# Three rotating PSUM banks for up products and a piece's products, one bank for products back and turned rows, in a fused selective-scan and mixture-of-experts kernel

## The chip, the core and the metric

The kernel runs on one core of a Trainium2 chip. The engines that matter are TensorE (PE, with its weight loads as PEld), VectorE (DVE), ScalarE (ACT), GpSimd (POOL, which here only issues indirect DMAs) and SyncE (SP, which issues plain DMAs). Each runs its own list of instructions in order and waits on semaphores for the others. TensorE writes only into PSUM; in this kernel PSUM is used as eight banks, each 128 partitions by 512 float32 numbers. The metric is the device time of one execution in microseconds; the median of three runs is given, and one more execution was profiled.

## The reference

The input x has 2 batches of 2048 tokens of 256 numbers. After a layer norm the output is the input plus two branches:

```
xn  = layernorm(x)
# branch 1: a selective scan over tokens sorted by their nearest of 8 means
buckets = argmax(normalized xn . normalized means)     # order = stable sort by bucket
u    = xn in that order, transposed                    # (B, 256, L)
dts, Bm, Cm = split(x_proj_weight @ u);  Cm += prompt of the bucket
delta = softplus(dt_projs_weight @ dts + bias)
h_t  = exp(delta_t * A) * h_{t-1} + (delta_t * u_t) * B_t      # 256 x 16 states
y_t  = sum over states of h_t * C_t + D * u_t          # put back in the old order
# branch 2: top 2 of 8 experts for each token
out  = sum over the two experts of p * (silu(xn @ w1) * (xn @ w3)) @ w2
x + branch 1 + branch 2
```

## The kernel before

**Front.** The rows of x are loaded, turned (`turn_rows`, L376: for each group of 512 tokens one half goes through a bank of pool `ps_m`, the other through `ps_t`, L379), scored against the 16 columns of means and gate weights (`by_chooser`, two banks of pool `ps_h`), normalised and written to a scratch tensor in DRAM. Tokens are routed to experts and sorted by bucket; `list_tokens` (L310) turns positions into lists of row numbers with products into the tile `pl`.

**Two streams of work, interleaved by hand.** After the front, two streams share the engines.

The *scan stream* has 8 pieces of 512 tokens (2 batches of 4). A piece has 8 steps (4 groups of 4 states, by 2 halves of the 256 channels), so there are 64 steps, and a step has 4 places. At a place VectorE multiplies du by B into `bu` (`feed`, L840) and runs one scan of 512 steps into `hs` (`scan`, L849), while ScalarE makes a decay `da` for the step after it (L834). TensorE works one step behind: at places 1 and 2 it turns the finished `hs` (`turn`, L861, into two banks of `ps_t`; ScalarE copies them out as `ht`, L865), and at place 3 it contracts with `z`, which holds C, into the two accumulators `y0` and `y1` (L870, the two banks of `ps_s`). Before a piece can begin, its rows are gathered, turned (`Piece.turn`, tile `pt_u`, L653), projected (`project` and `end_projection`, tile `px`, L667 and L674), and its step sizes made (`size`: products into two tiles `pd`, L714, then eight ScalarE passes into `e` and `r`, L732). All of this is done during the piece before it, at fixed places: `turn` at place 2 and 3 of that piece's step 1, `project` in two calls at places 1 and 3 of step 2, `end_projection` at place 0 of step 3, and `size` behind the first product back that is dealt from place 2 of step 3 on. `decay_of_one`, `log` and `series` (L734 to L757) follow in steps 4 to 7; `log` loads ScalarE's table for the logarithm.

The *expert stream* has 68 tiles of 128 token slots that are dealt among the places (three more tiles stand in a branch at the end, L1208, which this input doesn't take). A tile's rows are gathered by an indirect DMA (`load_rows`, L928), turned (`Tile.turn`, tile `pt_g`, L937, copied out as `xT`, L939), multiplied up by w1 and w3 (`up(0)` and `up(1)`, 16 products each into one bank, L954), gated on VectorE (`silu`, L967, after ScalarE's tanh, L962; `gate`, L971), multiplied back (`down`, tile `py`, L977), scaled on ScalarE (`yo`, L981) and added to the output by an indirect DMA (L895). Weights come by indirect DMAs too (L914), three tiles ahead. `Tile.turn` also makes `own`, each row's share, with two small VectorE instructions.

**PSUM.** `ps_s` has two banks (y0, y1), `ps_t` two (pt_s, and half of the front's turned rows). `ps_h` has one bank for each of two tags: `h0` for the product `up(0)` and `h1` for `up(1)`. `ps_m` has two banks that everything else shares in turn: `pt_g`, `py`, `pt_u`, `px`, `pd` and the small products of the front.

**The dealer.** The expert stream is a list of jobs: `up(0)` and `up(1)` of tile t, then `down` of tile t - 1, and so on (L1067 to L1072). Just before `down(t)` the job also turns the rows of tile t + 2 (`turn_tile`). The first seven jobs (`lead`, L1078) surround the first piece's preparation. The others are dealt in the loop over places: each place carries an estimate of its TensorE and VectorE time (`on_pe`, `on_dve`), and a job, at `PART` and `PART_DVE`, is given as soon as TensorE's sum falls behind a fixed ratio of VectorE's. A silu or gate is recorded two places after its product, in `later`; `vector_work(t)` records at once all that is left of tiles up to t. `part_up(t)` calls it for t - 1 before its products, `part_down(t)` for t. Finally `keep_order` fixes each engine's instructions in the order in which they were recorded.

Of the kernel before, what the change touches and what calls it, by code (L numbers as in the profile page):

```python
# [39 lines left out]
F32 = mybir.dt.float32  # L40
# [5 lines left out]
PSUM = bass.MemoryType.PSUM  # L46
DRAM = bass.MemoryType.DRAM

P = 128
# [7 lines left out]
def scan_moe_kernel(  # L57
# [46 lines left out]
    ps_t = ctx.enter_context(tc.tile_pool(name="ps_t", bufs=2, space=PSUM))  # L104
    ps_h = ctx.enter_context(tc.tile_pool(name="ps_h", bufs=1, space=PSUM))
    ps_m = ctx.enter_context(tc.tile_pool(name="ps_m", bufs=2, space=PSUM))
    front = ctx.enter_context(ExitStack())
# [193 lines left out]
    def first_of_max(v, m, i):  # L301
# [6 lines left out]
        nc.vector.tensor_reduce(i, c, AX.X, ALU.min)  # L308

    def list_tokens(place, of_batch, width: int, tag: str, factors, between=()):  # L310

# [10 lines left out]
        lo, hi = lo_hi  # L322
        pl = ps_m.tile([P, 2, width], F32, tag="m", name="pl")
        for m in range(n // LC):
# [41 lines left out]

    by_chooser = [ps_h.tile([P, CH], F32, tag=f"h{b}", name="by_chooser") for b in range(B)]
    scores = [ps_s.tile([P, JC, JC, G], F32, tag=f"y{b}", name="scores") for b in range(B)]
# [269 lines left out]
    class Piece:  # L638
# [9 lines left out]
        def turn(self, h: int):  # L648
            if h == 0:
                self.u = pre.tile([P, ND, CH], F32, tag="tok", name="u")  # L650
            pt = ps_m.tile([P, JC, P], F32, tag="m", name="pt_u")
            for i in range(JC):
                nc.tensor.transpose(pt[:, i, :], self.xs[:, i, h * P : (h + 1) * P], ident)  # L653
            nc.scalar.copy(self.u[:, h, :], pt.rearrange("p i t -> p (i t)"))
# [8 lines left out]
        def project(self, h: int):  # L663
            if h == 0:
                self.px = ps_m.tile([2 * XP, HC], F32, tag="m", name="px")
            for t in range(2):
                nc.tensor.matmul(  # L667
                    self.px[t * XP : (t + 1) * XP, :], lhsT=xpT[:, h, :],
                    rhs=self.u[:, h, t * HC : (t + 1) * HC], start=h == 0, stop=False,
                )  # L670
# [38 lines left out]
        def size_products(self):  # L709

            self.pd = [ps_m.tile([P, ND, HC], F32, tag="m", name="pd") for _ in range(2)]
            for h in range(ND):
                for t in range(2):
                    nc.tensor.matmul(  # L714
                        self.pd[t][:, h, :], lhsT=dtT[t * XP : t * XP + R, h * P : (h + 1) * P],
                        rhs=self.xd[t * XP : t * XP + R, :], start=True, stop=True,
                    )
# [191 lines left out]
    class Tile:  # L909
# [37 lines left out]
        def up(self, i: int):  # L947
            wk = w13_sb[self.t % NW][:, i * ND * H : (i + 1) * ND * H].rearrange(
                "p (h f) -> p h f", h=ND
            )  # L950
            p = ps_h.tile([P, NH, TS], F32, tag=f"h{i}", name=f"p{i}_ps")
            for f in range(NH):
                for h in range(ND):
                    nc.tensor.matmul(  # L954
                        p[:, f, :], lhsT=wk[:, h, f * P : (f + 1) * P], rhs=self.xT[:, h, :],
                        start=h == 0, stop=h == ND - 1,
                    )
            if i == 0:

                self.p1 = p  # L960
                self.s = ffn.tile([P, NH, TS], F32, tag="t", name="t_sb")
                nc.scalar.activation(self.s, p, AF.Tanh, scale=0.5)  # L962
            else:
                self.p3 = p
# [70 lines left out]
    def vector_work(t: int):  # L1035

        for when in sorted(later):
            later[when] = [(u, do) for u, do in later[when] if u > t or do()]

    def part_up(t: int, i: int):  # L1040
        def do():
            vector_work(t - 1)
            tiles[t].up(i)
# [5 lines left out]
    def part_down(t: int):  # L1049
        def do():  # L1050
            if t + 2 < n_dealt:
                turn_tile(t + 2)
            vector_work(t)
# [14 lines left out]
    for t in range(n_dealt + 1):  # L1068
        if t < n_dealt:
            jobs += [part_up(t, 0), part_up(t, 1)]  # L1070
        if t > 0:
            jobs.append(part_down(t - 1))  # L1072
    turn_tile(0)
    turn_tile(1)
# [42 lines left out]
    for n, p in enumerate(pieces):  # L1117
# [3 lines left out]
        if n:  # L1121
# [4 lines left out]
            for h in range(ND):  # L1126
                at_place(s1 + 1, 2 + h, lambda p=p, h=h: p.turn(h), 0.5)
                at_place(s1 + 2, 1 + 2 * h, lambda p=p, h=h: p.project(h), 0.55)
                at_place(s1, 18 + 2 * h, lambda p=p, h=h: p.decay_of_one(h))
# [21 lines left out]
    for n in range(NSUB * len(steps)):  # L1151
        on_dve[n] += 1.75
        if n >= NSUB:
            on_pe[n] += (0.0, 0.9, 0.9, 1.1)[n % NSUB]
    PART, PART_DVE = 2.05, 0.5
    left = len(jobs) - ahead
    ratio = (sum(on_pe[:n_places]) + left * PART) / (sum(on_dve[:n_places]) + left * PART_DVE)
    pe_now = dve_now = 0.0
    for k in range(len(steps)):
        step = steps[k]  # L1160
        before_ = steps[k - 1] if k else None
        for i in range(NSUB):
# [22 lines left out]
            while given < len(jobs) and (  # L1185
                pe_now + PART / 2 < ratio * dve_now or place + 1 >= n_places
            ):
                jobs[given]()
                given += 1
                pe_now += PART  # L1190
                dve_now += PART_DVE
                size_now()
# [89 lines left out]
```

## Time and profile before

| what | value |
|---|---|
| median of three runs | 751.91 us (751.2 to 751.93) |
| the profiled execution | 752.28 us |
| its span, first to last instruction | 750.5 us |
| mean granted TensorE clock | 0.951 |
| first bu of the scan stream | 98.66 us |
| end of the last dealt scan on VectorE | 735.2 us |

In the lists of waits a line names who waited, for what, and then the microseconds in total, how often, and the longest. In a timeline a line has its start, the time it spans, the engine, the source line, what was written from what, and how many like instructions are merged into it; the bracket at its end is idle time of that engine just before, with what ended it. In the table of stretches there follow, after the stretch and its length, busy time and instructions (x) of each engine, the granted clock, the DMA share and GB/s.

### The profile page before, as it was taken

The numbers are of one execution on the slowest core, as the hardware profiler recorded it, in microseconds if no ns is written. First come the engines' busy times: TensorE is split into PE (matmuls) and PEld (weight loads), VectorE is DVE, ScalarE is ACT, GpSimd is POOL, SyncE is SP. The second block draws the span as 40 slices with busy tenths as digits, with TensorE's granted clock in tenths as the row PEclk, the third lists the DMA queues.
The fourth block names the chain that finished last, engine by engine and source line by source line (L and its number), as shares of the span: only waits on it lengthen the run. The fifth ranks groups of instructions, "written<-read, shape, count | busy, mean of one in ns | idle before, by whom it ended". The sixth has DMA issues, their size and how long they took to land.

```text
span 750.5 us, 16877 instructions
## 1 busy us (share of the span) xinstructions
PE 678.0 (90%) x6506; PEld 588.9 (78%) x6506; DVE 678.5 (90%) x1085; ACT 508.0 (68%) x983; POOL 523.0 (70%) x362
## 2 busy tenths in 40 slices
PE   7375779999998999999999999999999998999993
PEld 5144678888877998888878898999798977899982
DVE  8885389899987999999999999999999997999991
ACT  4830446686758866886769577967795768767762
POOL 2023448667777788777877887788788888887733
PEclk9755979999999999999999999999999999999996
DMA  8676544584436755685458656865575547745312
GB/s 269 243 162 233 166 162 92 159 244 138 124 56 171 252 146 117 171 264 148 114 132 281 160 130 124 255 198 132 119 249 157 128 93 219 227 125 118 86 17 29
DMA packets 60401, 120.31 MB, mean 160 GB/s; under 512 B 24160, under 2 KB 41248, under 8 KB 53152
## 3 DMA queue, kind: packets, MB, share of 16 engines
q0 software_dynamic: 38784, 63.71, 36.0%
q1 hardware_dynamic: 21536, 55.50, 21.9%
q8 instruction: 52, 0.85, 0.5%
q14 instruction: 29, 0.24, 0.1%
HBM read 170.78 MB, written 22.28 MB: 257 GB/s over the span
## 4 chain that ended last, share of the span: by engine, by line
PE 69%; ACT 11%; DVE 9%; DMA 5%; issue 4%; POOL 1%; POOLq 0%; ACTq 0%; DVEq 0%
PE p_ps L954 29%; PE py L977 13%; PE pt_s L861 11%; PE y L870 7%; DMA w<-in_w_down_dram,w_row 3%; ACT ht L865 3%; PE y L796 2%; PE pl L342 2%; PE pt_g L937 2%; DMA out_dram<-yo,token_of 2%; ACT da L834 2%; DVE st L374 1%; ACT e L732 1%; ACT r L732 1%; PE px L667 1%
## 5 line engine op out<-in xcount | busy, mean ns | idle before, releaser
L954 PE MATMUL p_ps<-xT,w 128*128 128x128 f32 x2176 | 272.6, 281 | 12.3 <-DVE g L971 8.1
L954 PEld LDWEIGHTS p_ps<-xT,w 128*128 128x128 f32 x2176 | 258.0, 195 | 26.3 <-DVE g L971 8.3
L849 DVE TENSOR_TENSOR_SCAN hs<-da,carry,bu 128x512 f32<-128x512 f32 x192 | 246.0, 1281 | 0.0
L834 ACT ACTIVATE da<-dl,na 128x512 f32<-128x512 f32 x256 | 183.7, 734 | 0.2 <-DVE dl L789 0.2
L840 DVE TENSOR_TENSOR bu<-du,bt 128x512 f32<-128x512 f32 x256 | 173.1, 676 | 0.0
L865 ACT COPY ht<-pt_s 128x512 f32<-128x512 f32 x256 | 138.4, 595 | 40.3 <-PE pt_s L861 39.3
L895 POOL DMA_INDIRECT out_dram<-yo,token_of x68 | 131.4, 1932 | 48.0 <-ACT yo L981 22.6
L914 POOL DMA_INDIRECT w<-in_w_up_dram,w_row x68 | 91.8, 1350 | 89.2 <-DVE w_row L595 43.4
L861 PE MATMUL pt_s<-ident,hs 128*128 128x128 f32 x1024 | 136.8, 277 | 9.7 <-ACT ht L865 8.6
L977 PE MATMUL py<-w,g 128*128 128x256 f32 x544 | 129.8, 381 | 7.5 <-ACT xT L939 4.8
L861 PEld LDWEIGHTS pt_s<-ident,hs 128*128 128x128 f32 x1024 | 116.5, 142 | 21.4 <-ACT ht L865 13.4
L977 PEld LDWEIGHTS py<-w,g 128*128 128x128 f32 x544 | 98.0, 190 | 20.6 <-ACT xT L939 6.0
L928 POOL DMA_INDIRECT xg_sb<-xn,token_of x68 | 91.8, 1349 | 26.2 <-issue 12.8
L914 POOL DMA_INDIRECT w<-in_w_down_dram,w_row x68 | 94.7, 1392 | 20.7 <-issue 13.4
L895 POOL DMA_INDIRECT out_dram<-yt,line_of x32 | 66.1, 2065 | 23.0 <-issue 11.3
L849 DVE TENSOR_TENSOR_SCAN hs<-da,bu 128x512 f32<-128x512 f32 x64 | 78.1, 1221 | 0.0
L962 ACT ACTIVATE t_sb<-p_ps 128x512 f32<-128x512 f32 x68 | 41.0, 603 | 54.5 <-PE p_ps L954 54.4
L870 PE MATMUL y<-ht,z 128*32 128x128 f32 x2048 | 74.0, 277 | 1.5 <-PEq L1208 0.7
L981 ACT ACTIVATE yo<-py,own 128x256 f32<-128x256 f32 x68 | 32.3, 475 | 61.4 <-PE py L977 58.8
L967 DVE SCALAR_TENSOR_TENSOR t_sb<-t_sb,p_ps 128x512 f32<-128x512 f32 x68 | 45.8, 674 | 26.1 <-ACT t_sb L962 26.1
L870 PEld LDWEIGHTS y<-ht,z 128*32 128x32 f32 x2048 | 50.8, 109 | 19.6 <-issue 10.2
L632 POOL DMA_INDIRECT xs<-xn,line_of x32 | 41.8, 1306 | 14.7 <-issue 8.2
(202 smaller groups left out, 582.0 us busy)
## 6 DMA issues: line engine op xcount, KB each, us to landing
bt<-bc SPq DMA_DIRECT2D x31, 1024.0 KB, 5.1
z<-bc SPq DMA_DIRECT2D x32, 256.0 KB, 3.2
xn<-xt SPq DMA_DIRECT2D x8, 520.0 KB, 2.6
xt<-in_x_dram SPq DMA_DIRECT2D x8, 512.0 KB, 8.0
out_dram<-in_x_dram SPq DMA_DIRECT2D x8, 512.0 KB, 8.3
w<-in_w_up_dram,w_row POOLq DMA_INDIRECT x68
w<-in_w_down_dram,w_row POOLq DMA_INDIRECT x68
xg_sb<-xn,token_of POOLq DMA_INDIRECT x68
```

The source lines that it names most:

```text
L834: nc.scalar.activation(self.da[i], self.piece.dl[:, self.h, :], AF.Exp, scale=na[:, self.h, n : n + 1])
L840: nc.vector.tensor_mul(self.bu[i], self.piece.du[:, self.h, :], self.piece.bts[self.q][:, i, :])
L849: nc.vector.tensor_tensor_scan(self.hs[:, :, i], self.da[i], self.bu[i], start, ALU.mult, ALU.add)
L861: nc.tensor.transpose(pt[:, j, :], self.hs[:, t0 : t0 + G, :].rearrange("p t n -> p (t n)"), ident)
L865: nc.scalar.copy(self.ht[i], pt)
L870: nc.tensor.matmul(p.ys[self.h][j * G : (j + 1) * G, i, :], lhsT=p.zs[q][:, i * (P // G) + j, :], rhs=self.ht[i][:, j, :], start=False, st ...
L895: ins = nc.gpsimd.indirect_dma_start(out=out_rows, out_offset=bass.IndirectOffsetOnAxis(ap=numbers, axis=0), in_=rows, in_offset=None, com ...
L914: nc.gpsimd.indirect_dma_start(out=to[self.t % NW], out_offset=None, in_=rows, in_offset=bass.IndirectOffsetOnAxis(ap=w_row[:, self.t : se ...
L928: nc.gpsimd.indirect_dma_start(out=self.xg, out_offset=None, in_=xn_d, in_offset=bass.IndirectOffsetOnAxis(ap=token_of[:, self.t : self.t ...
L954: nc.tensor.matmul(p[:, f, :], lhsT=wk[:, h, f * P : (f + 1) * P], rhs=self.xT[:, h, :], start=h == 0, stop=h == ND - 1,)
L967: nc.vector.scalar_tensor_tensor(self.s, self.s, 1.0, self.p1, ALU.add, ALU.mult)
L977: nc.tensor.matmul(py, lhsT=self.g[:, f, :], rhs=w2[:, f, :], start=f == 0, stop=f == NH - 1)
```

## The change

`ps_h` becomes one ring of three banks under a single tag `h`. Besides the up products it takes `pt_u`, `px`, both `pd` tiles and `pl`; the front's two `by_chooser` tiles come from it as well. `ps_m` shrinks to one bank, which is left to `pt_g`, `py` and the small or turned tiles of the front.

A list `taken` remembers which tile's product lies in each of the three banks. `take_bank`, called ahead of every allocation from the ring, records all silu and gate work up to the tile whose product lay in the bank that now comes round. `part_up` no longer calls `vector_work` itself.

The rows of tile t + 1 are turned just before `up(1)` of tile t; before, those of tile t + 2 were turned just before `down(t)`. Both calls of `project` move to place 0 of step 3, next to `end_projection`. The dealer's estimates are replaced: a place's VectorE time, TensorE's three places, and a job's time, which now differs for up products and products back. A job's own time decides when it is given.

```diff
-    ps_h = ctx.enter_context(tc.tile_pool(name="ps_h", bufs=1, space=PSUM))
-    ps_m = ctx.enter_context(tc.tile_pool(name="ps_m", bufs=2, space=PSUM))
+    ps_h = ctx.enter_context(tc.tile_pool(name="ps_h", bufs=3, space=PSUM))
+    ps_m = ctx.enter_context(tc.tile_pool(name="ps_m", bufs=1, space=PSUM))
...
+    taken = [-1] * 3
+    vector_work_to = [lambda t: None]
+
+    def take_bank(t: int = -1):
+        vector_work_to[0](taken.pop(0))
+        taken.append(t)
...
-        pl = ps_m.tile([P, 2, width], F32, tag="m", name="pl")
+        pl = ps_h.tile([P, 2, width], F32, tag="h", name="pl")
+        take_bank()
...
-            pt = ps_m.tile([P, JC, P], F32, tag="m", name="pt_u")
+            take_bank()
+            pt = ps_h.tile([P, JC, P], F32, tag="h", name="pt_u")
...
-                self.px = ps_m.tile([2 * XP, HC], F32, tag="m", name="px")
+                take_bank()
+                self.px = ps_h.tile([2 * XP, HC], F32, tag="h", name="px")
...
-            self.pd = [ps_m.tile([P, ND, HC], F32, tag="m", name="pd") for _ in range(2)]
+            self.pd = []
+            for _ in range(2):
+                take_bank()
+                self.pd.append(ps_h.tile([P, ND, HC], F32, tag="h", name="pd"))
...
-            p = ps_h.tile([P, NH, TS], F32, tag=f"h{i}", name=f"p{i}_ps")
+            take_bank(self.t)
+            p = ps_h.tile([P, NH, TS], F32, tag="h", name=f"p{i}_ps")
...
+    vector_work_to[0] = vector_work
+
     def part_up(t: int, i: int):
         def do():
-            vector_work(t - 1)
+            if i == 1 and 1 < t + 1 < n_dealt:
+                turn_tile(t + 1)
             tiles[t].up(i)
...
     def part_down(t: int):
         def do():
-            if t + 2 < n_dealt:
-                turn_tile(t + 2)
             vector_work(t)
             tiles[t].down()
...
+    UP, DOWN, GATE, OWN = 2.0, 2.4, 0.67, 0.36
+    job_pe = [DOWN if n % 3 == 1 and n > 1 else UP for n in range(len(jobs))]
...
-                at_place(s1 + 2, 1 + 2 * h, lambda p=p, h=h: p.project(h), 0.55)
+                at_place(s1 + 3, 0, lambda p=p, h=h: p.project(h), 0.55)
...
-        on_dve[n] += 1.75
+        on_dve[n] += 1.95
         if n >= NSUB:
-            on_pe[n] += (0.0, 0.9, 0.9, 1.1)[n % NSUB]
-    PART, PART_DVE = 2.05, 0.5
-    left = len(jobs) - ahead
-    ratio = (sum(on_pe[:n_places]) + left * PART) / (sum(on_dve[:n_places]) + left * PART_DVE)
+            on_pe[n] += (0.0, 1.07, 1.07, 1.14)[n % NSUB]
+    left = sum(job_pe[ahead:])
+    left_dve = (len(jobs) - ahead) * (2 * GATE + OWN) / 3
+    ratio = (sum(on_pe[:n_places]) + left) / (sum(on_dve[:n_places]) + left_dve)
...
-                pe_now + PART / 2 < ratio * dve_now or place + 1 >= n_places
+                pe_now + job_pe[given] / 2 < ratio * dve_now or place + 1 >= n_places
             ):
                 jobs[given]()
+                pe_now += job_pe[given]
+                dve_now += (2 * GATE + OWN) / 3
                 given += 1
-                pe_now += PART
-                dve_now += PART_DVE
```

More of the change, by code (lines that the diff above doesn't have):

```diff
@@ L363, in late_factors @@
         return one, num
-    by_chooser = [ps_h.tile([P, CH], F32, tag=f"h{b}", name="by_chooser") for b in range(B)]
+    by_chooser = [ps_h.tile([P, CH], F32, tag="h", name="by_chooser") for b in range(B)]
     scores = [ps_s.tile([P, JC, JC, G], F32, tag=f"y{b}", name="scores") for b in range(B)]
```

## The prediction, made before the changed kernel had run

> **What bounds the kernel now.** I read five views in this order: the page's head, stretches of the dealt region, who waits on VectorE, who waits on TensorE, and the timeline around the longest waits.
>
> ```profile
> span 750.5 us, 16877 instructions
> PE 678.0 (90%) x6506; PEld 588.9 (78%) x6506; DVE 678.5 (90%) x1085; ACT 508.0 (68%) x983; POOL 523.0 (70%) x362
> ```
>
> Two engines stand at 90% of the span, so the stretches must tell which one ends the work.
>
> ```profile
> core 0: us, PE busy (x) PEld busy (x) DVE busy (x) ACT busy (x) POOL busy (x), PEclk, DMA share, GB/s
> ...
> 210.00:260.00 50.00, 45.80 (x429) 39.55 (x429) 42.03 (x59) 36.87 (x72) 39.07 (x24) 0.97 0.61 165
> ...
> 460.00:510.00 50.00, 49.88 (x506) 45.63 (x506) 49.59 (x71) 39.59 (x78) 40.97 (x27) 1.00 0.72 211
> ...
> 610.00:660.00 50.00, 46.05 (x461) 39.34 (x460) 44.29 (x61) 36.53 (x72) 42.07 (x27) 1.00 0.70 190
> ```
>
> Some stretches have both engines full (460 to 510); in others both lose time together (210 to 260, 610 to 660). VectorE's losses have one name:
>
> ```profile
> DVE t_sb L967 <- ACT t_sb L962: 26.1, 14, 4.4
> ...
> DVE one L327 <- PE pl L342: 3.2, 2, 2.3
> ```
>
> silu (L967) waits for the tanh (L962), which waits for an up product (L954). In VectorE's timeline the waits from the first scan's bu (98.7 us) to the last scan's end (735.2 us) are: 1.66 and 0.41 (silu and gate at 109 and 110), 2.31 and 0.99 (list_rows(1) at 133 and 136), 0.37, 0.31 and 0.34 (149, 190, 197), 3.26 (224), 4.43 (241), 1.32 (318), 2.05 (395), 0.84 (546), 1.61 (621), 3.82 (636): 23.7 us. Two of them:
>
> ```profile
> 224.44 0.69 DVE L967 SCALAR_TENSOR_TENSOR t_sb<-t_sb,p_ps 128x512 f32<-128x512 f32 x1 [3.26 <-ACT t_sb L962]
> ...
> 241.47 0.69 DVE L967 SCALAR_TENSOR_TENSOR t_sb<-t_sb,p_ps 128x512 f32<-128x512 f32 x1 [4.43 <-ACT t_sb L962]
> ```
>
> Start to start, VectorE takes 0.60 for a bu, 1.19 for a scan, 0.60 for a silu or gate and 0.31 for a tile's two own. One piece is 32 x 1.79 = 57.3, plus 8.2 tiles (197 dealt parts / 3 / 8) x 1.51 = 12.4, plus 7.2 of masks, series and members: 76.9 us. TensorE in the same way: a step 2 x 0.87 + 1.01 = 2.75, a tile 2 x 1.89 + 1.75 + 0.22 = 5.75, a piece's products 5.6; so 22.0 + 47.2 + 5.6 = 74.8 us. The pace is VectorE's, but TensorE has only 2.1 us a piece to spare, so each microsecond that TensorE waits soon returns as a silu that comes late. Without any VectorE wait the span would be 750.5 - 23.7 = 726.8: the floor.
>
> TensorE's own waits:
>
> ```profile
> PE pt_s L861 <- ACT ht L865: 8.6, 17, 2.2
> ...
> PE p_ps L954 <- DVE g L971: 8.1, 1, 8.1
> ...
> PE py L977 <- ACT xT L939: 4.8, 5, 1.4
> PE p_ps L954 <- ACT xT L939: 3.9, 5, 1.1
> PE py L977 <- ACT u L654: 2.6, 3, 1.2
> ```
>
> ```profile
> 98.19 3.78 PE L954 MATMUL p_ps<-xT,w 128*128 128x128 f32 x16 [8.07 <-DVE g L971]
> ```
>
> ```profile
> 215.79 0.38 PE L937 MATMUL pt_g<-ident,xg_sb 128*128 128x128 f32 x2
> 217.62 1.99 PE L977 MATMUL py<-w,g 128*128 128x256 f32 x8 [1.45 <-ACT xT L939]
> ```
>
> While px holds one of two ps_m banks (L665 to L679), the product back must take the bank of the rows just turned, and waits for ScalarE's copy. At 98 us the second up bank is held by tile 1's gate, which VectorE reaches only after the first piece's step sizes.
>
> **The change, part by part.**
>
> *Up products on three banks.* An up product now waits for the silu or gate three allocations back. In the first parts, pt_u's second half takes the bank of tile 1's first product, so silu and gate of tile 1 are forced ahead of it, into a time when VectorE idles (8.5 us before w, L775). The product of 98.19 then needs pd0's bank, whose last reader is the third of the four step-size r on VectorE, near 91.9: it starts 6.3 us sooner. The 1.66 + 0.41 at 109 go: -2.1. Gate 1 also leaves VectorE's way before the first bu (97.46): -0.6.
>
> The row at 98.19 shows 3.78 us for 16 matmuls, after 8.07 us without work and at a granted clock of 0.50; warm they take 1.95. The Trainium skill (TensorE: Matmul & The Clock Gate, Part 1) puts the drop at an idle window of about 3.4 us; the wait left would be some 1.9 us, so by it the product stays warm and saves 1.8 more. TensorE is already early there, so the sum is the same by either.
>
> *A piece's products leave ps_m; both project calls go to one place.* The py waits of 4.8 + 2.6 go. Piece by piece upstream of a VectorE wait: 1.45 at 129 (ahead of list_rows' products, ready before 131.5 but started at 132.75: takes 1.2 of 3.3); 1.22 + 1.45 at 206 and 217 (2.7 of 3.26); 0.72 at 297 (of 1.32); 0.71 at 375 (of 2.05); 0.65 at 526 (of 0.84); 0.70 + 0.46 at 603 and 615 (1.2 of 1.61). Sum: -7.2. Moving project (0.58 each) past other TensorE work adds none; its bank is held for some 2 us, not 10.
>
> *Rows turned one part sooner.* An xT copy now has a whole up product (1.89) ahead of its use, so the 3.9 us of up products waiting for xT go; one, 1.09 at 171, lies ahead of the three small waits: -0.7 of 1.0. On POOL's queue the row load (mean 1.35) now stands ahead of the up-weight load instead of behind it; both serve three tiles later, and TensorE waits for no weight or row DMA in this trace, so nothing; uncovered it is 1.35 a tile. own comes earlier on VectorE with the same 0.31; its rows are three tiles old. SP's queue keeps its order.
>
> *One bank for rows turned and products back.* Each is now separated from the other by an up product. From pt_g's start to the copied xT was 1.8 us at 215.79; pt_g plus an up product is 2.1. So it is hidden by 0.3, save where ScalarE loads the logarithm's table and runs it (1.28 + 1.06 at 251 us): there py comes 0.9 late, seven times, 6.3 us of TensorE. I take 0, as VectorE's series (four of 1.12 a piece) lies there and no wait stands between 250 and 315. Bounds: 0 and +6.3.
>
> The Trainium skill (PSUM — Partial Sum Buffer, Summary: rules for kernel authors) speaks against this part: reading a product while a matmul runs wants another bank. By it each of some 132 handoffs is in series, and only the order, not the bank, can hide it. The row at 217.62 agrees with the rule: 1.45 us where nothing lay between.
>
> *Front.* pt_x's first halves share one bank. TensorE must wait for ScalarE's copy (0.51 start to start) before every second tile: about 0.4 in each of three bursts, ahead of the normalising, which lies on the chain: +1.3 (bounds 0 and 3). At 70 us the second pt_g waits for the first copy, and pt_u stands behind a third: +0.9 until the first bu.
>
> *A size's gate forced sooner; parts dealt by new costs.* Walking both planners, 168 of 197 parts keep their place, 27 move by one, two by two; a place is 2.4 us and silu waits two places, so 0. Where size follows, pd's second bank can pull a gate one place forward: at most one silu distance, 1.1 us in piece 2, which the next silu then doesn't lose: 0, bounds 0 and +5. ScalarE's eight step-size passes (232.68 to 235.7), which hold ht back by 2.16 and make the 4.43 and 3.82, stay: 0.
>
> **Sum.** -2.1 - 0.6 - 7.2 - 0.7 + 1.3 + 0.9 = -8.4: span 742.1. The profiled execution took 752.28, 1.8 around its span, and 0.4 above the median 751.91. So 742.1 + 1.8 - 0.4 = 743.5; I say 743.
>
> **Rivals.**
>
> *More comes than was counted (13%).* TensorE is six microseconds early from the start and up products have a bank to run ahead in; nearly every silu is on time. For it: 2.1 us a piece to spare. Against it: the 2.16 of step-size passes is untouched. Only list_rows' 2 remain of 23.7, with the front's +2.2: about 731.
>
> *The waits move (15%).* VectorE runs dry at the next late silu or forced gate, and only the lead and list gain: -2.1 - 0.6 - 1.2 + 2.2 = -1.7: 750. For it: the two longest waits come from ScalarE, and the copy chain is longer now.
>
> *Slower: the one bank binds (22%).* Place: py behind xT and pt_g behind yo, two handoffs a tile over 66 tiles, on a ScalarE that also carries da and ht in order. Removed TensorE waits are 4.8 + 2.6 + 3.9 + 8.1 = 19.4, so from 0.3 us a tile TensorE is later than before. At 0.5 it loses 33, 14 more than it gained: 752 + 14 = 766; at 0.4, 759. For it: the hidden margin is just 0.3. Against it: in this trace ScalarE waits for py 59 times out of 68 (58.8 us), so it is seldom behind.
>
> That the third bank doesn't do what it says can be excluded but for a part: up products waited for a bank once only (8.1), so in the steady part its worth lies in freeing ps_m.
>
> **How the numbers follow.** The forecast's case has 50% and a range of its own of 735 to 748. Less than 0.2% (1.5 us) can't be told from no change. Faster: 50 + 13 and half of the case at 750: 71%. Same: the rest of it: 8% with a little of the slower one. Slower: 21%. The range takes in the case at 750 and the milder half of the slower one, and leaves out most of the case at 731: 734 to 757.
>
> **What would show it.** Right: no py wait on xT or u left, no 8 us wait at 98, silu's 26.1 near 15, the two waits after the step sizes still there, the first bu 1 to 2 us later. Wrong: py waiting on xT or pt_g on yo in most tiles (the slower case), silu's wait unchanged, or a front later by over 3 us.

## The result, and the profile after

| | before | after |
|---|---|---|
| median | 751.98 us (751.2 to 753.19, 6 runs) | 756.2 us (752.82 to 759.47, 6 runs) |
| ratio after / before | | 1.0058, 95% interval 1.0036 to 1.0080 |
| span of the profiled execution | 750.5 us | 755.0 us |
| first bu | 98.66 us | 100.77 us |
| end of the last dealt scan | 735.17 us | 738.07 us |

The changed kernel is 0.6% slower; 743 us and a gain of 1.2% were forecast. Here and below medians are of all executions, while ratios with their intervals leave out the slow ones, over 1.5% above the fastest of the same kernel.

The page's head and the three stretches shown of before, in the kernel after:

```profile
span 755.0 us, 16857 instructions
PE 677.1 (90%) x6506; PEld 592.8 (79%) x6506; DVE 679.3 (90%) x1085; ACT 508.2 (67%) x983; POOL 516.1 (68%) x362
```

```profile
210.00:260.00 50.00, 45.80 (x431) 39.92 (x429) 45.20 (x63) 37.72 (x73) 36.40 (x24) 0.97 0.63 173
460.00:510.00 50.00, 47.29 (x475) 43.20 (x475) 47.07 (x68) 37.23 (x74) 38.27 (x26) 0.97 0.72 205
...
610.00:660.00 50.00, 45.91 (x437) 40.63 (x436) 42.68 (x58) 38.53 (x75) 38.75 (x26) 0.97 0.65 182
```

From 210 to 260 VectorE gained three microseconds (42.03 to 45.20 busy). From 460 to 510, where both engines had been full, each now loses about 2.6, and the granted clock is no longer 1.00. So the change gains early and loses late. The start of the first scan of some steps says where (from VectorE's timeline in three traces; the third kernel, with one edit to the changed one, is explained under the experiments):

```
step                          0       4      12      36      48      52      60   last end
before                     99.86  145.65  227.42  466.13  585.04  622.34  703.59   735.17
after                     101.97  144.79  225.01  461.08  583.73  624.50  706.49   738.07
after, gather sooner      101.24  143.84  224.01  460.25  580.55  615.76  696.60   728.22
```

After is 2.1 us late at step 0 and 5.05 us early at step 36: 7.2 gained in the first half. By step 60 it is 2.9 us late. The waits of the whole execution, in the columns of before:

```profile
DVE t_sb L982 <- ACT t_sb L977: 26.1, 14, 4.9
...
PE pt_s L875 <- ACT ht L879: 11.2, 20, 2.6
...
PE py L992 <- ACT xT L953: 4.7, 6, 1.4
...
PE pt_u L663 <- DMA xs<-xn,line_of: 4.3, 1, 4.3
...
PE p_ps L969 <- DMA w<-in_w_up_dram,w_row: 2.1, 1, 2.1
...
DVE one L336 <- PE pl L351: 1.8, 2, 0.9
...
PE p_ps L969 <- DVE r L792: 1.6, 1, 1.6
```

What was to vanish has mostly vanished: the 8.1 us of an up product waiting for a gate, the 3.9 of up products waiting for xT, the 2.6 of py waiting for u. VectorE's wait for tanh is as long as before, and two names are new, both DMAs: TensorE waits for a piece's gathered rows (xs) and for a tile's up weights (w). The first of them, in TensorE's timeline:

```profile
599.35 0.49 PE L663 MATMUL pt_u<-ident,xs 128*128 128x128 f32 x3
604.16 0.48 PE L663 MATMUL pt_u<-ident,xs 128*128 128x128 f32 x1 [4.31 <-DMA xs<-xn,line_of]
...
607.34 2.61 PE L992 MATMUL py<-w,g 128*128 128x256 f32 x8
```

and in VectorE's, where the next silu then misses its place:

```profile
606.49 1.28 DVE L863 TENSOR_TENSOR_SCAN hs<-da,carry,bu 128x512 f32<-128x512 f32 x1
612.40 0.69 DVE L982 SCALAR_TENSOR_TENSOR t_sb<-t_sb,p_ps 128x512 f32<-128x512 f32 x1 [4.64 <-ACT t_sb L977]
```

VectorE's 4.64 us is put down to ScalarE's tanh. Followed back it is the DMA: tanh waited for an up product, which stood behind pt_u in TensorE's order. GpSimd's timeline shows when the rows were asked for:

```profile
595.33 1.25 POOL L641 DMA_INDIRECT xs<-xn,line_of  x1 [0.30 <-issue]
596.89 1.48 POOL L641 DMA_INDIRECT xs<-xn,line_of  x1 [0.31 <-issue]
598.67 1.61 POOL L909 DMA_INDIRECT out_dram<-yo,token_of  x1 [0.30 <-ACT ht L879]
600.59 1.38 POOL L928 DMA_INDIRECT w<-in_w_down_dram,w_row  x1 [0.30 <-issue]
602.28 1.40 POOL L942 DMA_INDIRECT xg_sb<-xn,token_of  x1 [0.31 <-issue]
```

Here one indirect DMA follows another with 0.30 us between them and nothing else. The last gather leaves GpSimd at 598.37, one microsecond before TensorE begins to turn its rows. The queue was no better in the kernel before: there the last gather left at 597.84, and TensorE came later, at 600.72. Even so the trace of before held a warning, small enough to be missed:

```profile
600.72 0.49 PE L653 MATMUL pt_u<-ident,xs 128*128 128x128 f32 x3
601.51 0.33 PE L653 MATMUL pt_u<-ident,xs 128*128 128x128 f32 x1 [0.30 <-DMA xs<-xn,line_of]
```

The lead of that gather over its use was 2.9 us before and 1.0 after. That is 1.9 of the 4.0 us by which the wait grew. The rest lies behind GpSimd: the rows were there 5.8 us after the gather had left it (598.37 to 604.16), against 3.7 before (597.84 to 601.51). In between stands another transfer, `bt<-bc`, a plain load of 1024 KB for the scan stream. SyncE issued it at these times, before and then after:

```profile
598.83 0.33 SPq L703 DMA_DIRECT2D bt<-bc  x1
```

```profile
597.58 0.33 SPq L714 DMA_DIRECT2D bt<-bc  x1
```

Before, the last gather left GpSimd 1.0 us ahead of this load; after, 0.8 us behind it, since the scan stream had come forward and the gather had not. The view of the DMA queues of the kernel after, from 598.40 to 601.00, has one queue alone, that of SyncE's plain DMAs (GpSimd's is q0; the line has packets, megabytes, share of the 16 DMA engines' time):

```profile
q1 hardware_dynamic: 115, 0.94, 97.9%
```

For 2.6 us after the last gather had left GpSimd, nothing that GpSimd had issued moved. TensorE's five waits on gathered rows over 0.4 us, in the traces of the changed kernel and its variants, are all of this kind: `bt` had gone out 0.8 to 1.9 us before the gather left GpSimd. No run moved `bt` by itself, so how much of the wait it makes is read from the traces alone.

The table of stretches shows GpSimd's queue itself, before first, then after (the fifth busy time and count are GpSimd's):

```profile
280.00:440.00 160.00, 156.22 (x1561) 137.04 (x1559) 155.63 (x216) 119.30 (x229) 127.78 (x83) 1.00 0.61 168
...
560.00:680.00 120.00, 113.36 (x1143) 99.82 (x1142) 113.63 (x159) 85.29 (x165) 101.24 (x61) 1.00 0.59 158
```

```profile
280.00:440.00 160.00, 156.77 (x1609) 140.00 (x1608) 157.53 (x218) 120.84 (x232) 128.34 (x83) 1.00 0.63 169
...
560.00:680.00 120.00, 109.95 (x1060) 99.14 (x1059) 109.33 (x153) 81.56 (x159) 97.11 (x63) 0.96 0.60 165
```

With 0.30 us behind every DMA, GpSimd was occupied for 127.78 + 83 x 0.30 = 152.7 of 160 us before, and for 101.24 + 61 x 0.30 = 119.5 of 120 us in the later stretch. "70% busy" on the page was there a full queue. It is not full everywhere: in another execution of the kernel before (before_look) the later stretch has 96.57 + 61 x 0.30 = 114.9 us, and in the kernel after 97.11 + 63 x 0.30 = 116.0. After the change TensorE and VectorE do more from 280 to 440 (1609 matmuls for 1561), and GpSimd issues the same 83 DMAs. Work that runs ahead eats up the lead of its own loads until it meets them: the smallest lead of a tile's up weights, from leaving GpSimd to their first use, was 12.4 us before and is 5.2 after.

### The profile page after: what moved, and what is told of

The parts are those of the page before. It is cut to its first block, busy times and chain, and to the rows that moved or that the text cites. A ratio compares the mean times of both kernels' runs of the same rounds, so it can differ in the third digit from the quotient of the medians.

```text
span 755.0 us, 16857 instructions
## 1 busy us (share of the span) xinstructions
PE 677.1 (90%) x6506; PEld 592.8 (79%) x6506; DVE 679.3 (90%) x1085; ACT 508.2 (67%) x983; POOL 516.1 (68%) x362
## 4 chain that ended last, share of the span: by engine, by line
PE 59%; DVE 14%; ACT 9%; DMA 8%; issue 6%; POOL 2%; POOLq 0%; ACTq 0%; DVEq 0%
PE p_ps L969 23%; PE py L992 11%; PE pt_s L875 9%; PE y L884 6%; DVE hs L863 4%; DMA w<-in_w_down_dram,w_row 3%; DVE bu L854 3%; ACT ht L879 2%; PE pl L351 2%; PE pt_g L951 2%; DMA out_dram<-yo,token_of 2%; DMA w<-in_w_up_dram,w_row 1%; PE y L810 1%; PE pt_x L391 1%; POOL out_dram L909 1%
## 5 line engine op out<-in xcount | busy, mean ns | idle before, releaser
L969 PEld LDWEIGHTS p_ps<-xT,w 128*128 128x128 f32 x2176 | 262.3, 197 | 10.1 <-issue 4.4
L909 POOL DMA_INDIRECT out_dram<-yo,token_of x68 | 135.1, 1987 | 67.9 <-ACT yo L996 35.4
L875 PE MATMUL pt_s<-ident,hs 128*128 128x128 f32 x1024 | 137.3, 277 | 11.3 <-ACT ht L879 11.2
L928 POOL DMA_INDIRECT w<-in_w_up_dram,w_row x68 | 88.9, 1307 | 85.4 <-DVE w_row L604 45.9
L992 PE MATMUL py<-w,g 128*128 128x256 f32 x544 | 131.5, 385 | 6.5 <-ACT xT L953 4.7
L909 POOL DMA_INDIRECT out_dram<-yt,line_of x32 | 61.6, 1927 | 18.2 <-issue 11.2
L986 DVE SCALAR_TENSOR_TENSOR g<-t_sb,p_ps 128x512 f32<-128x512 f32 x68 | 45.7, 672 | 5.7 <-PE p_ps L969 4.7
```

The source lines that it names most:

```text
L875: nc.tensor.transpose(pt[:, j, :], self.hs[:, t0 : t0 + G, :].rearrange("p t n -> p (t n)"), ident)
L909: ins = nc.gpsimd.indirect_dma_start(out=out_rows, out_offset=bass.IndirectOffsetOnAxis(ap=numbers, axis=0), in_=rows, in_offset=None, com ...
L928: nc.gpsimd.indirect_dma_start(out=to[self.t % NW], out_offset=None, in_=rows, in_offset=bass.IndirectOffsetOnAxis(ap=w_row[:, self.t : se ...
L969: nc.tensor.matmul(p[:, f, :], lhsT=wk[:, h, f * P : (f + 1) * P], rhs=self.xT[:, h, :], start=h == 0, stop=h == ND - 1,)
L992: nc.tensor.matmul(py, lhsT=self.g[:, f, :], rhs=w2[:, f, :], start=f == 0, stop=f == NH - 1)
```

## The experiments

Two theories at first. *The queue*: the change works, but TensorE and VectorE now catch up with GpSimd's gathers and weights. *The banks*: one ps_m bank, or a product forced into a new order, gives back what was gained, and the DMA waits only follow. Each set of runs had the kernel before beside it. In three sets that takes 752 us, in two others 768. Why they differ is not known: the record gives the same chip number to a set of 768.15 and to the one of 751.98. Ratios are always against the kernel before of the same set.

**Less work on GpSimd.** Both kernels without the expert stream's adds, 68 of GpSimd's 336 indirect DMAs.

```diff
             nc.scalar.activation(yo, py, AF.Copy, scale=self.own)
-            add_rows([(token_of[:, self.t : self.t + 1], yo)])
```

> The kernel before without the 68 indirect adds of the experts' rows (their part of the output is left out); this takes 68 instructions of some 2.2 us with their issue gap, about 150 us, off POOL's queue and nothing off TensorE, VectorE or ScalarE. Theory 1 (POOL's queue of indirect DMAs is a third engine at its limit, and the changed kernel runs into it): the kernel before sat just at that limit, so it gains little, 0 to 6 us (746 to 752). Theory 2 (the changed kernel's own PSUM waits on TensorE cost the time): nothing but the adds goes, the same range.

> The changed kernel without the 68 indirect adds of the experts' rows (their part of the output is left out). Theory 1 (POOL's queue): the weights are issued 15 us or more ahead of their use all through, TensorE waits for no row or weight DMA, and the time is 4 to 9 us below that of the kernel before with the same left out. Theory 2 (PSUM waits): the distance stays as it is with the adds in, 3 to 5 us above the kernel before with the same left out.

The kernel before takes 755.36 us without them, ratio 1.0011 (0.9977 to 1.0045): nothing gained, where 746 to 752 was forecast. The changed kernel takes 746.92, ratio 0.9912 (0.9882 to 0.9941), 8.4 us less than the kernel before without them, as the theory of the queue had it (4 to 9), and 9.3 less than its own 756.2, which is of another set. The stretch from 560 to 680 of the changed kernel without the adds:

```profile
560.00:680.00 120.00, 114.53 (x1153) 103.03 (x1152) 115.64 (x160) 85.48 (x169) 70.23 (x48) 0.99 0.43 134
```

GpSimd is occupied for 70.23 + 48 x 0.30 = 84.6 of 120 us, and no wait of TensorE on a DMA of the expert stream or of the pieces is left. So relief of this queue is worth nothing to the kernel before and much to the changed one. It takes load off the DMA engines too (their share falls from 0.60 to 0.43), so it does not tell GpSimd's queue from the transfers behind it.

**The gather two steps sooner.** All work stays; the four gathers of a piece are issued about 30 us earlier, in both kernels.

```diff
-            at_place(max(s1 - 1, 0), 1 if n > 1 else 0, p.gather)
+            at_place(max(s1 - 3, 0), 1 if n > 1 else 0, p.gather)
```

> The changed kernel with each piece's row gather (4 indirect DMAs) issued two steps sooner. Theory 1: the 4.3 us that TensorE waited for xs at 604 us go, but the weights behind the gather are issued later, so part returns as waits for weights: 751 to 755, and less spread between runs. Theory 2: no change, 755 to 757.

> The kernel before with each piece's row gather issued two steps sooner. If the sooner gather were simply a better place for any kernel (rival), this falls by as much as the changed kernel did with it (756.2 to 746.4, 10 us): 742 to 746. If it only takes away a wait that the change had made (theory 1), the kernel before, which waited 0.3 us for xs in all, stays within 751 to 753.5.

> The changed kernel with the sooner gather, beside the two others. Theory 1: 0.988 to 0.994, that is 10 us below the changed kernel and 6 below the kernel before with the sooner gather. Rival: no more than 3 us below the kernel before with the sooner gather.

> The kernel before with each piece's row gather two steps sooner, beside the changed kernel with and without it. Theory 1 (the change made the gather late): ratio 0.998 to 1.002 on a chip where the kernel before takes 751 to 753. Rival (a better place for any kernel): 0.985 to 0.992.

> The kernel before, unchanged, run as if it were another. Every theory: ratio 1.00, its interval holding 1. Its trace shows where the kernel before spends its time in these runs: if its median is near 752 as at first, the first bu is near 98.7 and the wait of pt_u on its gathered rows is under 0.5 us; if it is near 768, the 16 us more should be seen as waits of TensorE on gathered rows or on weights (then GpSimd's queue is what differs), or as a later first bu by 3 to 5 us.

> The kernel before with each piece's gather two steps sooner. A (the lateness is the change's own): a ratio of 0.997 to 1.00 wherever the kernel before takes 752. B (every kernel gains): 0.988 to 0.992 there too, as after gained 0.987 from the same edit.

> The changed kernel with the gather two steps sooner. A: 0.990 to 0.994 and at least 4 us under before_gather_3. B: within 2 us of before_gather_3.

| kernel before takes | before, gather sooner | after, gather sooner |
|---|---|---|
| 752.44 us | | 746.41 us, 0.9918 (0.9879 to 0.9957) |
| 768.4 us | 759.82 us, 0.9897 (0.9851 to 0.9943) | |
| 768.15 us | 760.7 us, 0.9927 (0.9889 to 0.9966) | 758.79 us, 0.9855 (0.9810 to 0.9900) |
| 752.47 us | 751.59 us, 0.9998 (0.9988 to 1.0008) | 745.86 us, 0.9909 (0.9891 to 0.9927) |

In the set of 752.47 the kernel before, run as if it were another, gave 1.0006 (0.9986 to 1.0026). There the sooner gather does nothing for it, and the changed kernel with it takes 745.86, 5.7 us under the kernel before with the same edit. So where the kernel before takes 752, the lateness is the change's own. The first forecast for the changed kernel, 751 to 755, was too cautious: no wait came back at the weights. And in the set of 752.44 moving four gathers a piece (746.41) gave as much as leaving out all the adds (746.92): a better place for these transfers was enough, and the queue's work could stay.

Two limits. The 10 us (756.2 to 746) are between sets; within one set of 752 the nearest comparison is the changed kernel with an extra bank in its front, below: 751.86, against 746.41 with the sooner gather. And in the one set where the changed kernel stood beside itself with the sooner gather, that of 768.15, the edit gained nothing: 758.31 and 758.79, 1.9 us under the kernel before with the same edit. 10 and 6 were forecast; what came is the rival's. In that set's trace of the changed kernel the last gather left 5.7 us ahead of its use and the 4.31 us wait is not there.

In the changed kernel with the gather sooner TensorE finds its rows:

```profile
596.25 0.60 PE L663 MATMUL pt_u<-ident,xs 128*128 128x128 f32 x4
597.79 0.66 PE L663 MATMUL pt_u<-ident,xs 128*128 128x128 f32 x4
```

Its steps 36 to 60 take 236.35 us instead of 245.41. In the sets of 768 the kernel before gains from the same edit, 0.7% to 1%.

The profiled execution of the last run, gather_sooner_3, was one of its longest, 755.42 us against a median of 745.86. From step 36 to 48 it took 129.36 us, where the first run of this kernel took 120.30; most of that was lost at one place:

```profile
500.29 3.78 PE L969 MATMUL p_ps<-xT,w 128*128 128x128 f32 x16 [6.90 <-DMA w<-in_w_up_dram,w_row]
```

```profile
490.13 1.97 POOL L942 DMA_INDIRECT xg_sb<-xn,token_of  x1 [0.30 <-issue]
492.40 1.01 POOL L928 DMA_INDIRECT w<-in_w_up_dram,w_row  x1 [0.30 <-issue]
```

In the first run of this kernel, whose span was 744.6, the same load of weights was issued 6.6 us sooner and left GpSimd 5.6 us sooner:

```profile
484.54 0.94 POOL L942 DMA_INDIRECT xg_sb<-xn,token_of  x1 [0.30 <-issue]
485.79 2.01 POOL L928 DMA_INDIRECT w<-in_w_up_dram,w_row  x1 [0.30 <-issue]
```

So the queue is still within a few microseconds of the work: in that first run the lead of the up weights over their use is 6.6 us at its smallest. In gather_sooner_3 the weights were there 6.9 us after they had left GpSimd (493.41 to 500.29), so an execution in which GpSimd falls behind by some 6 us pays at once.

**The front's turned rows on two banks.** Every second first half goes into a scan bank that is still free.

```diff
-            pool, tag = ((ps_m, "m"), (ps_t, "t"))[h]
+            pool, tag = (((ps_m, "m"), (ps_s, "y1"))[k % 2], (ps_t, "t"))[h]
...
-    scores = [ps_s.tile([P, JC, JC, G], F32, tag=f"y{b}", name="scores") for b in range(B)]
+    scores = [None] * B
...
         nc.scalar.copy(scT, by_chooser[b])
+        scores[b] = ps_s.tile([P, JC, JC, G], F32, tag=f"y{b}", name="scores")
```

> The changed kernel with the front's turned rows on a bank more (the odd groups' first halves go through y1's bank, which is idle in the front). Both theories: the first bu of the scan stream comes 1.5 to 2.5 us sooner than in the changed kernel (98.3 to 99.3). Theory 1: POOL sets the end, and most of it is taken back later, 755 to 756. Theory 2 or the front alone: the time falls by as much, 753.5 to 754.5.

> The changed kernel with the sooner gather and the front's extra bank. With the gather no longer late, the front's 1.7 us come through to the end: 743.5 to 745.5, against 746.4 with the sooner gather alone. If POOL still set the pace, it would stay at 746 to 747.

> The changed kernel with the gather two steps sooner and the front's turned rows on two banks. If the front's gain of 2.5 us in the first bu and the gather's gain add: 743.5 to 744.5 us where the kernel before takes 752 (0.988), and 2 us under the runs with the sooner gather alone (746). If the front's gain is lost at the next late thing: 746.

Alone: 751.86 us, 0.9983 (0.9944 to 1.0021), less than either forecast. The first bu comes at 98.25 instead of 100.77, and the work then meets its loads as before:

```profile
PE p_ps L970 <- DMA w<-in_w_up_dram,w_row: 2.7, 2, 1.8
...
PE pt_u L664 <- DMA xs<-xn,line_of: 1.6, 1, 1.6
```

In its profiled execution the last gather left GpSimd 1.0 us ahead of `bt` (596.53 and 597.52), and TensorE did not wait for it; the 1.6 us are of the piece before, where `bt` was ahead.

With the gather sooner as well: 757.94 us against 768.4, 0.9889 (0.9841 to 0.9936), and 746.13 against 751.98, 0.9927 (0.9895 to 0.9959; runs from 742.05 to 753.37). The sum of both gains, 743.5 to 744.5, was not reached: its profiled execution, at 753.37, again lost its time to up weights (6.6 us in two waits of TensorE).

**The row load behind the weights again.** The prediction costed the new order on GpSimd's queue at nothing; here it is undone.

```diff
-                turn_tile(t + 1)
+                tiles[t + 1].turn()
             tiles[t].up(i)
...
             if i == 1 and t + NW < n_dealt:
                 tiles[t + NW].load_up()
+            if i == 1 and 1 < t + 1 < n_dealt and t + 1 + NW < n_dealt:
+                tiles[t + 1 + NW].load_rows()
```

> The changed kernel with each tile's row load behind its up-weight load on POOL's queue, as before the change (the turning stays where the change put it). If the swapped order made POOL late, the xs wait near 604 us goes and the time is 748 to 752; if it is the scan and the products that run ahead of a queue with no time to spare, it stays at 754 to 757.

> The changed kernel with each tile's row load behind its up-weight load on POOL's queue, as before the change. If the swapped order made the gather late: 0.996 to 1.000. If it is the work that runs ahead of a queue with no time to spare: as the changed kernel, 1.003 to 1.008, with a wait for xs of 3 to 5 us left near 600 us.

> The changed kernel itself, as a control on the chip of this call. As first measured: 1.003 to 1.008 of the kernel before, with a spread of several us. On a chip on which the kernel before waits for its DMAs too (as in the call before this one, where it took 768 us), the ratio is near 1 or below.

758.4 us in the set of 768.4 (0.9896, 0.9845 to 0.9947) and 758.24 us in that of 768.15 (0.9860, 0.9816 to 0.9903), where the changed kernel itself takes 758.31 (0.9811, 0.9750 to 0.9873). The weights' waits go, and the gather's wait stays:

```profile
PE pt_u L663 <- DMA xs<-xn,line_of: 4.1, 1, 4.1
```

Both traces have `bt` 0.8 us ahead of the last gather, as the kernel after has. The order of row load and weights among themselves is worth nothing that shows here. The forecasts were made for a kernel before of 752 and fit neither set. And in the set of 768.15 the unaltered changed kernel is 1.9% *faster* than the kernel before; its six executions run from 750.34 to 769.78, so the size is uncertain. Its profile shows the same waits, TensorE 5.6 us on up weights and 1.5 on gathered rows; what the kernel before loses there can't be read, since none of its executions in these two sets was profiled. The kernel before with the sooner gather was: its scan stream begins 5 us later there (first bu at 102.20 and 102.47, against 97.30 in the set of 752.47), and that of the changed kernel with it 4.5 us later (104.58 against 100.04), so a good part of what these sets cost lies ahead of the dealt region.

**The old deal.** The new banks and order with the old estimates.

```diff
-    job_pe = [DOWN if n % 3 == 1 and n > 1 else UP for n in range(len(jobs))]
+    job_pe = [2.05] * len(jobs)
...
-        on_dve[n] += 1.95
+        on_dve[n] += 1.75
...
-            on_pe[n] += (0.0, 1.07, 1.07, 1.14)[n % NSUB]
+            on_pe[n] += (0.0, 0.9, 0.9, 1.1)[n % NSUB]
```

(and 0.5 for a job's VectorE time at both places).

> The changed kernel with the dealer's old estimates (2.05 and 0.5 a part, 1.75 a place and so on). 29 of 197 parts move by a place. Theory 1: within 2 us of the changed kernel, 754 to 758, since the pace of the tiles is the same. If the new estimates themselves cost the time, it falls to 750 or below.

768.44 us against 768.4, 1.0011 (0.9969 to 1.0053).

```profile
PE py L992 <- ACT xT L953: 11.3, 11, 3.9
...
PE p_ps L969 <- DMA w<-in_w_up_dram,w_row: 6.3, 4, 3.2
```

In that set the banks without the new deal gain nothing, where rows_behind, with the deal, took 758.4; TensorE waits 11.3 us for xT ahead of py, but 9.0 to 12.5 in other runs of these two sets as well. How much the deal brings where the kernel before takes 752 was not tried.

**The step sizes in two halves.** On top of gather and front: the eight ScalarE passes that hold back ht, four and four.

```diff
             self.size_products()
             self.step_size(0)
-            self.step_size(1)
+            later.setdefault(now + 1, []).append((NT, lambda: self.step_size(1)))
```

> The changed kernel with the sooner gather, the front's banks parted, and the eight step-size passes of a piece in two halves of four with a place between them, so that ScalarE's copies ht come between. If the burst still costs (VectorE's 3.3 and 3.0 us after it, TensorE's 2.56 on ht, twice): 4 to 5 us under the changed kernel with sooner gather and parted front, whose span less gather_sooner's was about -2 us; so some 5 to 7 us under gather_sooner_3, ratio near 0.984. If VectorE merely waits elsewhere: within 2 us of gather_sooner_3.

```profile
PE py L993 <- ACT xT L954: 10.2, 9, 2.6
...
PE pt_s L876 <- ACT ht L880: 7.9, 19, 1.1
```

750.44 us (743.93 to 753.83), 0.9964 (0.9937 to 0.9992), 4.6 us above gather_sooner_3: neither forecast. Against the trace of that run TensorE's wait on ht falls by 3.3 us (11.2 to 7.9), and that of py on xT rises from 5.6 to 10.2: here the new order on ScalarE mostly changes who waits. Its fastest execution is near that of the sooner gather (743.68); its median is worse.

**The adds one job cycle later.** On top of gather and front: each tile's add is issued after a later tile's up weights, when yo has long been made.

```diff
-            add_rows([(token_of[:, self.t : self.t + 1], yo)])
+            unadded.append((token_of[:, self.t : self.t + 1], yo))
...
                 tiles[t + NW].load_up()
+            if i == 1:
+                add_made()
```

> The same kernel with each tile's add issued one job cycle later, behind the up-weight load of a later tile, when its yo has long been made. If the waits on yo at the head of GpSimd's queue narrow the weights' lead: GpSimd's wait for yo falls from some 30 us to under 5, the smallest lead of an up weight over its use rises from 7 to over 10 us, and the times have no stray runs near 750; the median 0 to 2 us under front_and_gather_2. If GpSimd's time goes into the instructions themselves: the lead stays at 6 to 8 us and the medians agree within 1 us. If the later add runs into the loads that follow: the lead falls.

```profile
POOL out_dram L910 <- ACT yo L1003: 3.0, 4, 1.3
```

749.4 us (748.85 to 750.14), 0.9968 (0.9956 to 0.9981), 3.3 us above front_and_gather_2, where the forecasts had 2 below to 1 above. GpSimd's wait for yo falls from 27.8 us there to 3.0, and the smallest leads of the up weights stay at 5 and 6 us (tiles 36 to 44). But the queue as a whole gained nothing: from the first bu to 715 us GpSimd's idle time beyond 0.30 us ahead of each DMA is 46.5 us without this edit and 44.6 with it, as it now waits longer ahead of the scan stream's adds (19.2 us, 9.1 without). So whether such waits narrow the lead is not settled by this run, and why it is slower is not shown.

The best kernel found is the changed one with the sooner gather: 0.991 of the kernel before in both sets of 752 in which it ran, with single executions 6 to 10 us longer. The kernel before has such executions too: 8 of 30 took 755 to 761 us in the set of 752.44.

## Why the prediction was wrong

The step that failed is a cost put at nothing: "TensorE waits for no weight or row DMA in this trace, so nothing". Its premise was off by a little: one wait of 0.30 us on gathered rows stood in the trace of before. The sum took 8 us out of the time of two engines and asked of the third, GpSimd's queue, only whether it was late now, not by how much it was early. It never named the gather of a piece's rows. What the runs showed in its place: a cost of some 10 us (756.2 with the gather at its place, 746.41 and 745.86 with it sooner in other sets; in the traces 9.1 us between steps 36 and 60: some 2 at a wait for weights, 5.6 from step 48 to 52, where the gather's wait of 4.31 stands, the rest scattered). The work came forward and its loads did not; the last gather, 0.5 us later than before, fell behind the 1024 KB of `bt`, which had come forward with the scans. The numbers were at hand: 101.24 us busy and 61 gaps of 0.30 in 120 us, and a lead of 2.9 us at the last piece that 5 us of progress must use up. The Trainium skill (Perfetto Trace Analysis, What "DMA-bound" means) lists, among what a DMA-bound kernel can be bound on, the issuing engine's sequencer, whose track is then solid with DMA instructions. The trace of before agrees for the stretch in which GpSimd was occupied for 119.5 of 120 us, at a DMA share of 0.59. It is not the whole of the 4.31 us wait, in which the DMA engines themselves were 97.9% busy for 2.6 us.

That 756.2 still lies within 734 to 757 is luck: the upper end stood for the one bank binding.

The other steps, judged where the queue is out of the way (the changed kernel with the sooner gather):

- *Up products on three banks: right.* The 8.07 us wait became this (in the kernel after), and VectorE's 1.66 and 0.41 at 109 and 110 us are gone:

```profile
94.23 2.05 PE L969 MATMUL p_ps<-xT,w 128*128 128x128 f32 x16 [1.56 <-DVE r L792]
```

  The wait left was put at 1.9, and the 16 matmuls take 2.05 us, not 3.78.
- *A piece's products and rows turned sooner: right in kind, mis-sized.* The waits on u and of p_ps on xT went. From the first bu to the last scan VectorE's waits fell from 23.7 to 16.1 us, and the time from the first scan to the last one's end from 635.3 to 627.0: -8.3, where the terms for it made -10.0 (-2.1, -7.2 and -0.7). The difference lies at one place: TensorE, early now, stands 4.80 us before the products of list_rows, its next 16 up products take 3.76 us instead of 1.95, and the silu at 149 us comes 2.01 late, where 0.37 was lost before. That the one makes the other is read from the order, not tested.
- *One bank for rows turned and products back: right.* By the rule cited there every handoff would have stood in series; the order hides nearly all of them. What is left is 5.6 us of py on xT, in six waits and mostly at the logarithm's places, where the prediction saw seven of 0.9. The mark "no py wait on xT left" was too strong.
- *Front: right in the main.* +2.2 was forecast, and -0.6 for gate 1; the first bu came 2.1 later in the kernel after and 1.4 in this one. Two banks gave 2.5 back. Of this up to a microsecond is chance: three executions with the front of before began list_rows' first product at 38.59, 39.80 and 38.87.
- *Step sizes: right.* The 4.43 and 3.82 stayed, as 3.31 and 3.02; taking the burst apart moved the wait to py.

Sum of these in that trace: +1.4 up to the first scan, -8.3 to the end of the last, and +1.0 behind it, for which there was no term: a span of 744.6 for the 742.1 forecast. Of the rivals, "the one bank binds" named the right sign for the wrong reason (its own waits come to 5.6 us). None of them was the case that happened: a transfer that had been hidden by 2.9 us.

What stays open: the sign itself. The changed kernel was measured as slower in one set of 752, and in the set of 768.15 it is 1.9% faster. A sooner gather helps the kernel before there and not the changed one, so its own lead of 2.9 us may be what the kernel before has lost; without a trace of it this is argued, not shown.

## What to carry to other kernels

Before costing a gain on the two busy engines, list for every queue of DMA issues the lead of each issue over its use, and the share of time in which the queue is occupied, gaps included: the smallest lead bounds how much of the gain can be kept. Ask of that transfer, too, which other load the gain brings forward with it, since the two may change places on the DMA engines. The first remedy is the position of the one transfer with the smallest lead; here it was worth as much as leaving out 68 of the queue's 336 DMAs.

## What was not expected of the hardware

- GpSimd never issued two indirect DMAs closer than 0.30 us, whatever it waited for; 85 such gaps ahead of weight loads alone come to 25.9 us in the kernel after.
- The same indirect DMA occupies GpSimd for very different times. The four gathers of each piece in the kernel after (minimum, median and maximum in ns):

```profile
L641 POOL DMA_INDIRECT xs<-xn,line_of x32: 942/1253/1948, 72.2 to 596.9; - x32
```

  While VectorE stands idle early in the kernel they take 0.95 to 1.0 us; among the scans the row and weight loads take about 1.4 in the median. How much of an instruction a scan covers says little of it: over all 236 loads the correlation is 0.42 before and 0.29 after. The Trainium skill (SBUF — State Buffer, Who interferes with whom) has VectorE instructions with two SBUF inputs contend with GpSimd's reads, and infers that descriptor generation does not suffer from them. No run here took the scans away, so what makes the loads longer is not shown.
- A TensorE wait is dearer than its length: behind the 6.90 us wait the next 16 matmuls took 3.78 us instead of 1.95, behind 2.12 us 3.15, behind 1.56 us 2.05.
- The kernel before takes 752 us in some sets and 768 in others, and the order of the two kernels turns round between them.
- One plain load of 1024 KB kept what GpSimd had issued off the DMA engines for 2.6 us.
